# A gated recurrence on one core: the first input, state and biases come in two transfers instead of six, and the input products move one step later

## The chip, the core and the metric

The kernel runs on one core of a Trainium2 chip. Its time is the device time of one execution in microseconds (us). The profile calls the engines PE (TensorE, with PEld for its weight loads), DVE (VectorE), ACT (ScalarE), POOL (GpSimd) and SP (SyncE, which here only issues transfers).

## The reference, cut to what matters

There are 8 sequences of 512 steps, and 512 features and 512 states, all float32. One step needs the state that the step before it left, so the 512 steps are a chain.

```python
def step(h, x_t):
    fused = sigmoid(concatenate([x_t, h], -1) @ w_W + w_b)      # w_W: 1024 x 1024
    r, z = split(fused, 2, axis=-1)
    m = x_t @ wx_W + wx_b + r * (h @ wh_W + wh_b)               # wx_W, wh_W: 512 x 512
    h_new = z * h + (1 - z) * tanh(m)
    return h_new, h_new
out = x + scan(step, h0)                                        # over the 512 steps
```

The names in the kernel: r is the gate that multiplies the state's product, z the gate that keeps the old state. `x` is 8 x 512 x 512, and `h0` (called `cond_1024` in the inputs) is 8 x 512.

## The kernel before

**Layout.** The 512 units stand as four quarters of 128 partitions. The state is kept twice, as half A (quarters 0 and 1) and half B (quarters 2 and 3), in the tiles `hTA` and `hTB`, eight of each in turn. A product has 32 columns of state or of x as its stationary side and a row block of weights as its moving side, so four of them, for j = 0 to 3, fill the 128 partitions of one PSUM bank. Such a set of four is one "piece" below.

**The h side.** Each step i makes six pairs of pieces, in the order `ORDER = "R0 R1 G0 G1 R2 R3 G2 G3 H0 H1 H2 H3"`: R, G and H are three PSUM banks (with a second set for the next group), and the digit is the quarter of the state. The weights are `wgr` (for R and G) and `whh` (for H). DVE then transposes the banks into the state's layout (`turned`, `turn_h`; lines 292 and 310), ACT applies the sigmoids and the tanh (line 192), and DVE forms the new state by scans (line 272). Half A of the new state is ready before half B. POOL adds x and writes the output tile (line 375), and SP stores it every 16 steps.

**The x side.** The products of x don't depend on the state. Four steps make a group (`GS = 4`), and `prefill(g)` makes the group's four pieces (k = 0 to 3, from `wx`) into one of two PSUM banks `xps[g % 2]`, which `seed(g)` on ACT has filled with the biases before. `spread` copies the parts of `xps` into the banks R, G and H of the coming group (ACT, line 217), and `turn_x` transposes the part that belongs to `x_t @ wx_W` (DVE, line 222). Both run during the four steps of group g for group g + 1: at step s of a group, `turn_x(g + 1, s)` and the s-th of `spread`'s copies, or `seed(g + 3)` where s is 3, are the last things that DVE and ACT do. The pieces of `prefill(g + 2)` are made one per step, after the H products, where PE would otherwise wait for half A of the new state:

```python
        if s == 0:
            pre = prefill(g + 2) if g + 2 < NG else iter(())
        ...
        if i:
            take(pre, 1)
```

**The start.** Step 0 is special. Its x products are made in full before it (`both[0]`), and its R and G products go straight into `xps[0]` as one product called Q, 256 columns wide. Group 1's four x pieces are put between them: `FIRST = "Q0 x Q1 Q2 x Q3 x x H0 H1 H2 H3"`. The first piece of group 2 follows at the end of step 0. A bias product (`ones` times `rows4`) adds the biases to both `xps` banks, and DVE copies one of them into the SBUF tile `bias` (line 237), from which `seed` takes them later. Ahead of this PE makes six small products of zeros (tile `none`) and two 128 x 512 products of zeros, one into each `xps` bank; these set the banks' start.

**The transfers of the start.** ACT issues x of the first eight steps (`load_x(0, 0)`), h0 (`hin`), and four rows of biases, six in all. SP issues `wx` in four parts (3.1 MB together), `wgr` in four (2.1 MB), `whh` in two (1.0 MB), the second eight steps of x, and then the next chunks of 16 steps. In the instruction listing each transfer has one of eight completion semaphores, given out in turn, and a transfer that gets a semaphore which an earlier one still uses waits on its issuing engine until that one has landed.

The scheduling is by hand (`manual_schedule`): every engine runs its instructions in the order of the program's text.

Of the kernel before, what the change touches and what calls it, by code (L numbers as in the profile page):

```python
# [7 lines left out]
F32 = mybir.dt.float32  # L8
# [5 lines left out]
P = 128  # L14
NQ = 4
GS = 4
B = 8
# [8 lines left out]

ORDER = "R0 R1 G0 G1 R2 R3 G2 G3 H0 H1 H2 H3"

FIRST = "Q0 x Q1 Q2 x Q3 x x H0 H1 H2 H3"

BANKS = ("R", "G", "H")

# [4 lines left out]
def tile_cond_rnn_residual(  # L37
    ctx: ExitStack,
    tc: tile.TileContext,
    x: bass.AP,  # L40
    h0: bass.AP,
    wx_d: bass.AP,
    wgr_d: bass.AP,
    whh_d: bass.AP,
# [31 lines left out]
    nc = tc.nc  # L76
    NCH = x.shape[0]
    T = NCH * TC
    NG = T // GS

    const = ctx.enter_context(tc.tile_pool(name="const", bufs=1))
# [4 lines left out]

    xins = {}

    def load_x(c, half=slice(0, 2)):

        if c < NCH:
            if c not in xins:
                xins[c] = xin_p.tile([P, 2, NQ, TC * B // 2], F32, tag="xin", name=f"xin_{c}")
            (nc.scalar if half == 0 else nc.sync).dma_start(
                out=xins[c][:, half], in_=x[c].rearrange("p (e k n) -> p e k n", e=2, k=NQ)[:, half]
            )

    def x_of(c, k, t, n):

        e, t = divmod(t, TC // 2)  # L100
        return xins[c][:, e, k, t * B : (t + n) * B]

    load_x(0, 0)

    rows4 = const.tile([P, 512], F32, name="rows4")
    nc.vector.memset(rows4, 0.0)
    for j in range(NQ):
        nc.scalar.dma_start(out=rows4[32 * j : 32 * j + 1], in_=bias_d[j : j + 1])
    hin = const.tile([P, NQ, B], F32, name="hin")
    nc.scalar.dma_start(out=hin, in_=h0)  # L110

    wx = const.tile([P, NQ, NQ, 384], F32, name="wx")
    for k in range(NQ):
# [2 lines left out]
    wgr = const.tile([P, NQ, NQ, 256], F32, name="wgr")  # L116
    for k in range(NQ):
        nc.sync.dma_start(out=wgr[:, k], in_=wgr_d[:, k])
    whh = const.tile([P, NQ, NQ, 128], F32, name="whh")
# [3 lines left out]
    def wh(bank, k, j):  # L123
        return whh[:, k, j] if bank == "H" else wgr[:, k, j, {"G": slice(0, 128), "R": slice(128, 256), "Q": slice(0, 256)}[bank]]

    load_x(0, 1)

    def pair(n, name, rows, slots):
# [13 lines left out]
    zeros = const.tile([P, 512], F32, name="zeros")  # L142
# [4 lines left out]
    ones = const.tile([P, NQ, 32], F32, name="ones")  # L147
# [21 lines left out]
    xps = [psum.tile([P, 512], F32, name=f"xp{q}") for q in range(2)]  # L169

    def mm(out_, lhsT, rhs, start=False):
        nc.tensor.matmul(  # L172
            out_, lhsT, rhs, start=start, stop=False, skip_group_check=True
        )


    for t_ in list(banks[0].values()) + list(banks[1].values()):
        mm(t_, none[:, :128], none, start=True)
    for t_ in xps:
        mm(t_, zeros[:, :128], zeros, start=True)  # L180
    for hf in range(2):
        for slot in (0, 2):
            nc.vector.tensor_copy(
# [14 lines left out]
    def seed(g):  # L198

        nc.scalar.copy(xps[g % 2], bias)  # L200

    def prefill(g):

        c, t0 = divmod(g * GS, TC)
        for k in range(NQ):
            for j in range(NQ):
                mm(
                    xps[g % 2][32 * j : 32 * j + 32, 64:448],
                    x_of(c, k, t0, GS),
                    wx[:, k, j, :],  # L210
                )
            yield

    def spread(g, names):

        for n in names:
            nc.scalar.copy(banks[g % 2][n], xps[g % 2][:, XP[n]])  # L217
# [8 lines left out]
    def take(it, n=None):  # L226
        while n is None or n > 0:
            if next(it, it) is it:
                return
            n = None if n is None else n - 1  # L230

    both = [prefill(g) for g in range(2)]
    take(both[0], 2)
    for t_ in xps:
        mm(t_, ones.rearrange("p j m -> p (j m)"), rows4)
    bias = const.tile([P, 512], F32, name="bias")
    nc.vector.tensor_copy(bias, xps[1])
    take(both[0])
    spread(0, "RGH")
    for e in range(NQ):  # L240
        turn_x(0, e)
# [2 lines left out]
    for i in range(T):  # L244
        g, s = divmod(i, GS)
        c, t = divmod(i, TC)
        ps = banks[g % 2]
        if t == 0 and c > 0:
            load_x(c + 3)
        if t == 0:  # L250
            ot = out_p.tile([P, TC, NQ, B], F32, tag="ot", name=f"ot_{c}")
        if s == 0:
            pre = prefill(g + 2) if g + 2 < NG else iter(())

        for n in (ORDER if i else FIRST).split():
            if n == "x":
                take(both[1], 1)
                continue
            bank, k = n[0], int(n[1])
            hs = hT[k // 2][i % NH][:, :, k % 2, 2]  # L260
            for j in range(NQ):
                to = xps[0][:, :256] if bank == "Q" else ps[bank]
                mm(to[32 * j : 32 * j + 32, :], hs, wh(bank, k, j))
        if i:
            take(pre, 1)

        rows = slice(B * s, B * s + B)

# [77 lines left out]
        if i == 0:  # L346

            seed(2)
            take(pre, 1)
        if i == T - 1:  # L350
            nc.gpsimd.tensor_tensor(
                ot[:, t, :2, :].rearrange("p c n -> p n c"),
                x_of(c, slice(0, 2), t, 1).rearrange("p c n -> p n c"),
                state(0, T),
                ALU.add,
            )
# [17 lines left out]
        def add(hf, engine):  # L374
            return engine.tensor_tensor(  # L375
                ot[:, t, 2 * hf : 2 * hf + 2, :].rearrange("p c n -> p n c"),
                x_of(c, slice(2 * hf, 2 * hf + 2), t, 1).rearrange("p c n -> p n c"),
                state(hf, i + 1),
                ALU.add,
            ).ins  # L380
# [84 lines left out]
```

## Time and profile before

| | |
|---|---|
| median of 3 runs | 1697.41 us (1697.31 to 1697.63) |
| the profiled execution, its own time | 1697.74 us |
| its span, first to last instruction | 1695.9 us |
| busy: PE, PEld, DVE, ACT, POOL | 1683.5, 1463.7, 1093.9, 927.1, 231.1 us |
| moved by DMA | 30.86 MB, mean 18 GB/s |
| mean granted TensorE clock | 0.998 of full |
| first R product of step 1 | 24.11 us after the span's start |

All places in time below are microseconds from the start of the span. Between the span and the execution's own time lie 1.84 us that the profile doesn't show. In the chain of waits an entry is "start, length, what"; in the timeline it is "start, length, engine, line, operation, output and input, count", and a bracket at its end tells how long the engine stood idle before it and what ended that. The windows view gives, for each stretch, its length, PE's busy time, the number of PE's instructions, the granted TensorE clock as a share of full speed, the mean busy share of the 16 DMA engines, and GB/s.

### The profile page before, as it was taken

Reading aid. Unit: us, or ns where it says so; the run is one execution under the profiler, and the core shown is the slowest. Engines: PE = TensorE matmul, PEld = TensorE weight load, DVE = VectorE, ACT = ScalarE, POOL = GpSimd, SP = SyncE. Lnnn points to the kernel's source line nnn. Section 1 sums busy time; section 2 is a strip of 40 time slices with the busy share of each in tenths; the row PEclk is TensorE's granted clock in tenths of the full one; section 3 lists DMA queues with packets and bytes.
Section 4 is the critical chain, followed back from the end, with each engine's and each line's share of the span. In section 5 each row is a group of like instructions: output and inputs, shape, how many; then the busy total and the mean of one; then the engine's idle time right before and its main releaser. Section 6 shows DMA issues by size and latency. Waiting matters only on the chain.

```text
span 1695.9 us, 121388 instructions
## 1 busy us (share of the span) xinstructions
PE 1683.5 (99%) x53230; PEld 1463.7 (86%) x53230; DVE 1093.9 (65%) x8229; ACT 927.1 (55%) x5120; POOL 231.1 (14%) x1032
## 2 busy tenths in 40 slices
PE   8999999999999999999999999999999999999998
PEld 5888888888888888888888888888888888888887
DVE  4666666666666666666666666666666666666666
ACT  3555555555555555555555555555555555555554
POOL 0111111111111111111111111111111111111111
PEclk9999999999999999999999999999999999999999
DMA  4000000000000000000000000000000000000000
GB/s 176 17 4 17 17 17 17 12 9 17 17 17 17 5 17 17 17 17 4 17 18 17 17 10 11 17 17 17 17 4 17 17 17 17 4 17 11 11 11 10
DMA packets 11628, 30.86 MB, mean 18 GB/s; under 512 B 1364, under 2 KB 1876, under 8 KB 11096
## 3 DMA queue, kind: packets, MB, share of 16 engines
q1 hardware_dynamic: 10800, 22.94, 4.1%
q8 instruction: 416, 6.82, 1.7%
q14 instruction: 116, 0.95, 0.2%
q10 hardware_dynamic: 296, 0.16, 0.0%
HBM read 14.70 MB, written 8.39 MB: 14 GB/s over the span
## 4 chain that ended last, share of the span: by engine, by line
PE 98%; DMA 1%; DVE 0%; ACT 0%; issue 0%; SPq 0%
PE R L172 26%; PE G L172 26%; PE H L172 26%; PE xp L172 20%; DMA wx<-in_wx_dram 0%; DMA xin<-in_x_dram 0%; DVE md1A L310 0%; DVE hTA L272 0%; ACT hd0A L192 0%; ACT hTA L192 0%; DVE tz L292 0%; DVE md1A L222 0%; SPq L114 0%; ACT hTB L192 0%; ACT R L217 0%
## 5 line engine op out<-in xcount | busy, mean ns | idle before, releaser
L172 PE MATMUL xp<-wx,xin 128*32 128x384 f32 x4096 | 439.1, 488 | 2.4 <-DMA wx<-in_wx_dram 2.4
L172 PEld LDWEIGHTS R<-wgr,hTA 128*32 128x32 f32 x8176 | 243.5, 136 | 211.4 <-DVE hTA L272 211.0
L292 DVE STREAM_TRANSPOSE tr<-R 128x64 f32<-128x64 f32 x1022 | 194.4, 229 | 301.8 <-PE R L172 301.8
L172 PE MATMUL R<-wgr,hTA 128*32 128x128 f32 x8176 | 330.4, 273 | 2.6 <-DVE hTA L272 2.6
L172 PE MATMUL H<-whh,hTA 128*32 128x128 f32 x8192 | 330.7, 273 | 0.0
L172 PE MATMUL H<-whh,hTB 128*32 128x128 f32 x8192 | 330.7, 273 | 0.0
L172 PE MATMUL R<-wgr,hTB 128*32 128x128 f32 x8176 | 330.1, 273 | 0.0
L172 PE MATMUL G<-wgr,hTB 128*32 128x128 f32 x8176 | 330.1, 273 | 0.0
L172 PE MATMUL G<-wgr,hTA 128*32 128x128 f32 x8176 | 330.0, 273 | 0.0
L375 POOL TENSOR_TENSOR ot<-xin,hTB 128x16 f32<-128x16 f32 x511 | 127.7, 250 | 1457.2 <-DVE hTB L272 1362.4
L192 ACT ACTIVATE hd0B<-tz 128x16 f32<-128x16 f32 x512 | 115.5, 226 | 306.0 <-DVE tz L292 306.0
L172 PEld LDWEIGHTS H<-whh,hTA 128*32 128x32 f32 x8192 | 260.3, 136 | 0.3 <-issue 0.3
L172 PEld LDWEIGHTS G<-wgr,hTA 128*32 128x32 f32 x8176 | 259.7, 136 | 0.0
L192 ACT ACTIVATE md0A<-tr 128x16 f32<-128x16 f32 x512 | 120.8, 236 | 253.3 <-DVE tr L292 253.3
L172 PEld LDWEIGHTS H<-whh,hTB 128*32 128x32 f32 x8192 | 253.4, 122 | 0.0
L172 PEld LDWEIGHTS G<-wgr,hTB 128*32 128x32 f32 x8176 | 252.9, 122 | 0.0
L172 PEld LDWEIGHTS R<-wgr,hTB 128*32 128x32 f32 x8176 | 238.3, 122 | 0.1
L272 DVE TENSOR_TENSOR_SCAN hTA<-hd0A,hTA 128x48 f32<-128x48 f32 x512 | 132.1, 258 | 150.8 <-ACT hTA L192 150.8
L272 DVE TENSOR_TENSOR_SCAN hTB<-hd0B,hTB 128x24 f32<-128x24 f32 x1024 | 158.2, 196 | 103.0 <-ACT hTB L192 103.0
L192 ACT ACTIVATE hd0A<-tz 128x16 f32<-128x16 f32 x512 | 119.0, 232 | 110.8 <-DVE tz L292 110.8
L310 DVE STREAM_TRANSPOSE md1A<-G 128x64 f32<-128x64 f32 x511 | 160.6, 314 | 28.7
L192 ACT ACTIVATE hTB<-hTB 128x16 f32<-128x16 f32 x512 | 121.4, 237 | 82.3 <-DVE hTB L272 79.3
(58 smaller groups left out, 1679.1 us busy)
## 6 DMA issues: line engine op xcount, KB each, us to landing
xin<-in_x_dram SPq DMA_DIRECT2D x31, 256.0 KB, 3.8
out_dram<-ot SPq DMA_DIRECT2D x31, 256.0 KB, 2.9
wx<-in_wx_dram SPq DMA_DIRECT2D x4, 768.0 KB, 6.1
wgr<-in_wgr_dram SPq DMA_DIRECT2D x4, 512.0 KB, 8.6
whh<-in_whh_dram SPq DMA_DIRECT2D x1, 768.0 KB
whh<-in_whh_dram SPq DMA_DIRECT2D x1, 256.0 KB
out_dram<-ot SPq DMA_DIRECT2D x1, 192.0 KB
xin<-in_x_dram ACTq DMA_DIRECT2D x1, 128.0 KB, 5.2
```

The source lines that it names most:

```text
L172: nc.tensor.matmul(out_, lhsT, rhs, start=start, stop=False, skip_group_check=True)
L192: inst = nc.scalar.activation(out_, in_, func, **kw).ins
L272: nc.vector.tensor_tensor_scan(*[t_[:, :, c_].rearrange("p n c s -> p (n c s)") for t_ in (out_, d0, d1)], 0.0, ALU.mult, ALU.add,)
L292: inst = nc.vector.transpose(t_.rearrange("p c n -> p (c n)"), raw[n][hf]).ins
L310: nc.vector.transpose(md1[hf][g % 2][:, :, :, 0].rearrange("p n c -> p c n"), raw["h"][hf])
L375: return engine.tensor_tensor(ot[:, t, 2 * hf : 2 * hf + 2, :].rearrange("p c n -> p n c"), x_of(c, slice(2 * hf, 2 * hf + 2), t, 1).rearr ...
```

## The change

Six things are edited.

1. x of the first eight steps and h0 are packed side by side in one DRAM tensor `xh` and come in one transfer into a tile `head`. The products and the output additions of these steps read `head`.
2. The four rows of biases come in one transfer into partitions 0, 32, 64 and 96 of `rows4`.
3. The bias product goes into `xps[0]` alone, ahead of the x products, and starts that bank. DVE copies it to `bias` from there, and `seed(1)`, on ACT, copies the biases into `xps[1]`.
4. The two products of zeros in front both go into `xps[1]`; a third one (`warm()`) stands after group 0's x products.
5. In step 0 one x piece is taken out of `FIRST`, and it is the one piece at the end of the step. All x pieces now come from one sequence, `x_side()`: group g + 2's pieces are made at steps 4g + 1 to 4g + 4 instead of 4g to 4g + 3.
6. All transfers of `load_x` are issued by SP.

```diff
-FIRST = "Q0 x Q1 Q2 x Q3 x x H0 H1 H2 H3"
+FIRST = "Q0 x Q1 Q2 Q3 x x H0 H1 H2 H3"
...
+    NX = NQ * TC * B // 2
+    head = const.tile([P, NX + NQ * B], F32, name="head")
+    nc.scalar.dma_start(out=head, in_=xh)
+    hin = head[:, NX:].rearrange("p (k b) -> p k b", k=NQ)
...
-            (nc.scalar if half == 0 else nc.sync).dma_start(
+            nc.sync.dma_start(
...
         e, t = divmod(t, TC // 2)
+        if c == 0 and e == 0:
+            first = head[:, :NX].rearrange("p (k n) -> p k n", k=NQ)
+            return first[:, k, t * B : (t + n) * B]
         return xins[c][:, e, k, t * B : (t + n) * B]
 
-    load_x(0, 0)
 
     rows4 = const.tile([P, 512], F32, name="rows4")
     nc.vector.memset(rows4, 0.0)
-    for j in range(NQ):
-        nc.scalar.dma_start(out=rows4[32 * j : 32 * j + 1], in_=bias_d[j : j + 1])
-    hin = const.tile([P, NQ, B], F32, name="hin")
-    nc.scalar.dma_start(out=hin, in_=h0)
+    nc.scalar.dma_start(out=rows4[0:128:32], in_=bias_d)
...
-    for t_ in xps:
-        mm(t_, zeros[:, :128], zeros, start=True)
+    def warm():
+
+        mm(xps[1], zeros[:, :128], zeros)
+
+    mm(xps[1], zeros[:, :128], zeros, start=True)
+    warm()
+    mm(xps[0], ones.rearrange("p j m -> p (j m)"), rows4, start=True)
+    bias = const.tile([P, 512], F32, name="bias")
+    nc.vector.tensor_copy(bias, xps[0])
...
-    both = [prefill(g) for g in range(2)]
-    take(both[0], 2)
-    for t_ in xps:
-        mm(t_, ones.rearrange("p j m -> p (j m)"), rows4)
-    bias = const.tile([P, 512], F32, name="bias")
-    nc.vector.tensor_copy(bias, xps[1])
-    take(both[0])
+    def x_side():
+        for g in range(1, NG):
+            yield from prefill(g)
+
+    seed(1)
+    take(prefill(0))
+    warm()
+    later = x_side()
...
-        if s == 0:
-            pre = prefill(g + 2) if g + 2 < NG else iter(())
...
-                take(both[1], 1)
+                take(later, 1)
...
-        if i:
-            take(pre, 1)
+        take(later, 1)
...
             seed(2)
-            take(pre, 1)
```

More of the change, by code (lines that the diff above doesn't have):

```diff
@@ L40, in tile_cond_rnn_residual @@
     x: bass.AP,
-    h0: bass.AP,
+    xh: bass.AP,
     wx_d: bass.AP,
@@ L446 @@
     xd = c_(xd).reshape(NCH, 128, 4 * TC * Bn)
-    h0_d = c_(units(f["cond_1024"].T))
+    h0 = units(f["cond_1024"].T).reshape(128, 4 * Bn)
+    xh_d = c_(_np.concatenate([xd[0, :, : 2 * TC * Bn], h0], 1))
     nc = _bacc.Bacc("TRN2", target_bir_lowering=False, num_devices=1)
@@ L451 @@
     for name, a in (
-        ("x", xd), ("h0", h0_d), ("wx", wx_d), ("wgr", wgr_d), ("whh", whh_d), ("bias", bias_d),
+        ("x", xd), ("xh", xh_d), ("wx", wx_d), ("wgr", wgr_d), ("whh", whh_d), ("bias", bias_d),
     ):
```

## The prediction

> **What bounds the kernel now.** I read the page first: PE is busy 99% of the span, and its chain is "PE 98%; DMA 1%". In the timeline one step with its x piece takes 3.27 us of uninterrupted PE work (R starts at 1663.16 and 1666.43), so 512 steps are about 1670 us, which the change does not shorten. What it touches is the start, so next I read the chain of waits, its first 25 us (start, length, what):
>
> ```profile
> 0.74 5.23 DMA xin<-in_x_dram
> 5.99 0.33 SPq L114
> 6.36 7.07 DMA wx<-in_wx_dram
> 13.47 1.30 PE xp L172 x8
> 15.42 0.34 DVE md1A L222 x2
> 16.03 6.75 PE xp L172 x64
> 22.78 0.87 PE H L172 x32
> 23.65 0.64 PE xp L172 x8
> ```
>
> The last part of `wx` is issued only at 6.36, after the transfer of x, and lands at 13.43; then PE works through group 0's last piece and step 0, and step 1's R begins at 24.11 (timeline). Who made SP wait is in the waits of SP's queue (total, times, longest):
>
> ```profile
> SPq L114 <- DMA xin<-in_x_dram: 4.4, 1, 4.4
> SPq L118 <- DMA hin<-in_h_dram: 1.1, 1, 1.1
> ```
>
> By the instruction listing the third part of `wx` needs the completion semaphore that x's transfer holds: eight semaphores, and x, two parts of `wx`, h0 and four bias rows have all eight. The windows show what that does (fourth column the clock, last GB/s):
>
> ```profile
> 6.00:7.00 1.00, 1.00 (x9) 1.00 0.89 354
> 7.00:8.00 1.00, 0.75 (x12) 1.00 0.95 139
> 8.00:9.00 1.00, 1.00 (x9) 1.00 0.89 362
> 13.00:14.00 1.00, 0.53 (x8) 0.89 0.95 361
> 14.00:15.00 1.00, 0.75 (x8) 0.50 0.98 401
> 20.00:21.00 1.00, 1.00 (x16) 0.70 1.04 391
> ```
>
> The queue runs dry at 7 to 8. And PE, waiting for `wx`, loses half its clock from about 13.8 (0.89 of that window) to 20.6 (0.70).
>
> **Two transfers for six.** In the changed listing x with h0, the bias rows, four `wx` and two `wgr` parts share the eight semaphores, so all of `wx` is issued without a wait; the ninth, `wgr` part 2, waits for x, with some 3 MB queued ahead of it. What stays behind on SP's queue is the rest of `wgr`, `whh` and the later x, each waiting for a transfer long queued. The gain: issue plus time to landing gives 7.7 for `wx` part 1, 5.99 + 5.6 = 11.6 for part 2, 13.4 for part 3. Part 2 took 3.9 us after part 1, part 3 took 1.8 after part 2, at equal size. Without the dry queue part 2 should take 1.8 as well: 2.1 us saved, for all that lies behind. Bounds: at least the bytes missing in window 7 to 8, (400 - 139) of 400 GB/s, 0.65 us, if the late landings come from slow queues and not from the restart; at most 2.9, if also `wgr` part 0 (13.4 to 7.89 + 7.5 = 15.4, where parts 1 to 3 average (9.5 + 9.6 - 15.4)/3 = 1.2) loses its extra 0.8. I take 2.1, since parts 2 and 3 differ in nothing but the restart.
>
> So `wx` is complete at 11.3 instead of 13.4. `wgr` part 3 landed at 19.1, the second x at 11.6 + 10.4 = 22.0; between them 1.18 MB in 2.9 us, so `whh` part 0 was at 21.0 and part 1 at 21.7. After: `wgr` at 13.3, 14.5, 15.8 and 17.0, `whh` at 18.9 and 19.6.
>
> A rule of the Trainium skill speaks against this gain: "DMA: Bandwidth & Descriptors", section "Issuing engines are not separate DMA queues", says that transfers of all engines share the same 16 DMA engines and that spreading their issue saves only issuing time. By it the merge would be worth at most ACT's issue time, which no engine on the chain waits for: the sum would be left with the x piece below, 0.6 us. The 4.4 us wait on a semaphore's earlier user is another cost than that, so I go by the row.
>
> **Step 0.** With `wx` at 11.3, group 0's last piece takes 0.85 (row at 11.64, full clock); from its end to the first Q lie 1.29 (14.74 to 16.03: three copies, four transposes), so Q0 starts at about 13.5. At full clock Q pieces are 0.43 and x pieces 0.64: Q0 and x to 14.6, Q1 to 15.0, Q2 waits for its weights to 15.8, Q3 to 17.0 and ends at 17.4, two x pieces to 18.7, H waits for `whh` to 18.9 and its last quarter to 19.6. That quarter is 0.22 (of 0.87 for H), the x piece behind it 0.64: R of step 1 at 20.5 instead of 24.11. **3.6 us** gained. Here arrival of weights is what is late next; PE is not. So the x piece taken out of step 0 and the better clock are not added: they are what makes room for the weights to show. The state's path has slack: from Q3's end to half A of the new state it took 1.8 us (21.3 to 23.08), so 19.2, before 20.5.
>
> **Bias first.** The bias product now stands ahead of the x pieces on PE, and DVE's copy of it, 0.69, ahead of both h0 copies and of the first x piece, which must wait for it since it writes the same bank. The rows' landing isn't shown: x, ahead of them on ACT's queue, landed at 5.97, h0 behind it at 7.9. I take 6.4, where PE ends the zeros (2.69 + 3.72), because the rows now follow x directly: product 1.2, copy 0.7, three x pieces 1.9, so 10.2, and 1.1 us spare before 11.3. At 7.9 it would be 11.6, 0.3 late, hidden again by Q2's wait. Cost nothing; without that cover up to 0.9.
>
> **The zeros.** Two 128x512 zero products as before, hidden as before (PE waited for x). The third one, 0.85 to 1.86, lies in the 1.29 us between the last x piece and Q0: nothing at full clock, 0.6 at half, also ahead of Q2's wait. `seed(1)` on ACT, 0.59, is due by 12 and can run at 9. Nothing.
>
> **The x side one step later.** Step 504 gets a piece: steps without one last 3.23 (1669.60 to 1672.83), so **0.04** is lost. Every group's last piece now ends shortly before `turn_x` reads it on DVE, with ACT's copy of R and POOL's output additions behind: piece ends at 1643.79, `turn_x` ran at 1644.33, 0.54 spare. Nothing, unless that is used up. The bank's `seed` gets a step more.
>
> **Sum.** Span 1695.9 - 3.6 + 0.04 = 1692.3; with the 1.84 around it 1694.2; the profiled execution was 0.33 above the median, so the median should be 1693.8. A difference of about 0.2% (3.4 us) is what a measurement of this kernel can tell from no change, and the forecast lies just beyond it.
>
> **The rivals.** *The late queues stay late* (chance 0.11): only 0.65 us of arrival comes back, `whh` ends at 21.05, R starts at 21.9, gain 2.2 less 0.04: 1695.3. For it: `wgr` part 0 was slow without any dry queue. Against: parts 1 to 3 then ran evenly.
>
> *The clock falls in another stretch* (0.07). Before, a stretch of 3.4 us up to 13.8 with PE about a third busy ended at half clock, and one about 60% busy did not end it. After, 10.4 to 13.8 is about half busy, 13.8 to 17.2 as well. If the first drops the clock, the second is then full (Q and x at double length end at 17.2) and nothing is lost. If only the second does, 17.2 to 20.6 runs at half: two x pieces 2.6, H 1.2, R at 22.1, gain 2.0: 1695.4. "TensorE: Matmul & The Clock Gate", section "What's actually happening", has windows of 3.4 us and half clock only after an idle one; the 6.8 us in the trace are two of them, but a third of a window busy did not save the clock here, so the trace decides. By the page alone this rival could not happen.
>
> *Slower: DVE waits for the late piece* (0.06). `turn_x` stands in order before DVE's next transposes; if its piece ended over 0.54 us later than I read (a piece that waits, or a modelled end), 127 groups would each lose the excess, less the 0.6 us that DVE idles next. At an excess of 0.7, 0.1 x 127 = 13 us less the gain: 1707. Against: PE has no waits in these steps.
>
> **How the numbers follow.** The forecast has 0.76: from 1692.9 (weights 2.9 us earlier, so R at 19.7 and a gain of 4.4, and 0.1 more, as the lowest run lies 0.1 under the median) to 1694.8 (weights 1.1 us earlier, gain 2.6). Of it I give 0.66 to below 1694.0, as 2.1 is the mid of its bounds, and 0.10 to between. The range, 1692.9 to 1695.6, takes in the two smaller gains. Faster 0.66; same 0.10 + 0.11 + 0.07 = 0.28; slower 0.06.
>
> **What would show it.** Right: SP's first wait is at `wgr`, no window between 3 and 20 falls below 200 GB/s, `wx` lands near 11.3, R of step 1 starts near 20.5, steps keep 3.27. Wrong: a part of `wx` landing after 12.5; half clock past 18; DVE waits at `turn_x` in each group; R of step 1 bounded by PE rather than `whh`.

## The result, and the profile after

| | before | after |
|---|---|---|
| median of 22 runs | 1697.39 us | 1694.68 us |
| ratio | | 0.9985, 95% interval 0.9978 to 0.9992 |
| profiled execution: own time, span | 1697.74, 1695.9 us | 1694.75, 1693.0 us |
| R of step 1 starts | 24.11 us | 20.75 us |

The kernel is faster by 2.7 us, 0.15%. One of the 22 executions of the kernel before took 6329 us and stands outside the ratio. The first R product of step 1, before and after (timelines):

```profile
24.11 0.63 PE L172 MATMUL R<-wgr,hTA 128*32 128x128 f32 x16
20.75 0.62 PE L177 MATMUL R<-wgr,hTA 128*32 128x128 f32 x16
```

The chain of waits of the changed kernel, its first 21 us (start, length, what):

```profile
0.74 5.16 DMA head<-in_xh_dram
5.92 0.33 SPq L123
6.29 10.94 DMA wgr<-in_wgr_dram
17.27 1.95 PE xp L177 x24
19.22 1.07 PE H L177 x32
20.29 0.65 PE xp L177 x8
```

`wx` has left the chain. The wait for x's semaphore is still there (1.8 us in the waits of SP's queue), but the transfer that stands behind it is now part 2 of `wgr` (issued at 5.9, landed at 16.0), and the part issued next, the last of `wgr`, lands at 17.2. Meanwhile the queue has other parts to move. The windows:

```profile
6.00:7.00 1.00, 0.70 (x2) 1.00 1.02 424
7.00:8.00 1.00, 0.99 (x2) 1.00 1.05 442
11.00:12.00 1.00, 0.67 (x8) 1.00 0.96 233
14.00:15.00 1.00, 1.00 (x20) 1.00 1.03 418
20.00:21.00 1.00, 1.00 (x31) 1.00 0.87 326
```

The dry stretch at 7 to 8 is gone (442 instead of 139 GB/s), and no window from 14 to 21 shows half clock. (The first event of the clock is at 7.1 us in this trace; before it the view shows 1.00, although the products run at half speed.) One dip is left, 233 GB/s at 11 to 12, where part 0 of `wgr` is on its way. PE's timeline shows how step 0 now goes:

```profile
11.34 0.85 PE L177 MATMUL xp<-wx,head 128*32 128x384 f32 x8 [0.42 <-DMA wx<-in_wx_dram]
13.61 0.67 PE L177 MATMUL xp<-wgr,hTA 128*32 128x256 f32 x8 [0.37 <-DMA wgr<-in_wgr_dram]
17.27 0.66 PE L177 MATMUL xp<-wgr,hTB 128*32 128x256 f32 x8 [0.60 <-DMA wgr<-in_wgr_dram]
19.61 0.68 PE L177 MATMUL H<-whh,hTB 128*32 128x128 f32 x16
20.11 0.83 PE L177 MATMUL xp<-wx,head 128*32 128x384 f32 x8
```

The last piece of group 0 starts when `wx` is complete, at 11.34; every Q then starts when its part of `wgr` has landed. The last part of `whh` (issued at 7.6, 12.2 to landing) is there at 19.8, and R starts 0.95 behind it; before, R stood 2.4 behind it (21.7 and 24.11).

### The profile page after: what moved, and what is told of

Read it like the earlier page. It is cut to its first block, busy times and chain, and to the rows that moved or that the text cites. A ratio compares the mean times of both kernels' runs of the same rounds, so it can differ in the third digit from the quotient of the medians.

```text
span 1693.0 us, 121258 instructions
## 1 busy us (share of the span) xinstructions
PE 1681.5 (99%) x53230; PEld 1468.8 (87%) x53230; DVE 1087.5 (64%) x8229; ACT 916.6 (54%) x5121; POOL 230.3 (14%) x1032
## 4 chain that ended last, share of the span: by engine, by line
PE 98%; DMA 1%; DVE 0%; ACT 0%; issue 0%; SPq 0%
PE R L177 26%; PE G L177 26%; PE H L177 26%; PE xp L177 19%; DMA wgr<-in_wgr_dram 1%; DMA head<-in_xh_dram 0%; DVE md1A L320 0%; DVE hTA L282 0%; ACT hd0A L204 0%; ACT hTA L204 0%; DVE tz L302 0%; SPq L123 0%; ACT hTB L204 0%; DVE hTB L282 0%; ACT hd0B L204 0%
## 5 line engine op out<-in xcount | busy, mean ns | idle before, releaser
L177 PE MATMUL xp<-wx,xin 128*32 128x384 f32 x4032 | 432.4, 486 | 0.0
L177 PEld LDWEIGHTS R<-wgr,hTA 128*32 128x32 f32 x8176 | 248.9, 135 | 205.2 <-DVE hTA L282 204.7
L177 PEld LDWEIGHTS R<-wgr,hTB 128*32 128x32 f32 x8176 | 246.5, 122 | 0.0
L320 DVE STREAM_TRANSPOSE md1A<-G 128x64 f32<-128x64 f32 x511 | 157.1, 307 | 28.7
## 6 DMA issues: line engine op xcount, KB each, us to landing
whh<-in_whh_dram SPq DMA_DIRECT2D x1, 256.0 KB, 12.2
```

Source lines behind the costliest of these rows:

```text
L177: nc.tensor.matmul(out_, lhsT, rhs, start=start, stop=False, skip_group_check=True)
L320: nc.vector.transpose(md1[hf][g % 2][:, :, :, 0].rearrange("p n c -> p c n"), raw["h"][hf])
```

## The experiments

The theory: the gain is the earlier arrival of the weights, since SP issues all of `wx` without waiting for a completion semaphore. The rivals: fewer transfers are cheaper in themselves; PE's new order and its clock make the gain. All times are medians of 10 or 11 runs; the intervals of the ratios are about 0.09% to each side, or 1.5 us, so that medians tell a gain of 2.5 us from none, and smaller differences are read in the profiles, from one execution each. The three columns on the right are places in the profile, in us.

| kernel | median, us | ratio to before, interval | `wx` complete | last of `whh` | R of step 1 |
|---|---|---|---|---|---|
| merge alone | 1694.97 | 0.9986 (0.9977 to 0.9995) | 11.2 | 20.1 | 21.31 |
| PE's order alone | 1696.55 | 0.9996 (0.9987 to 1.0005) | 13.6 | 21.8 | 22.69 |
| no late zeros | 1694.78 | 0.9986 (0.9977 to 0.9995) | 11.3 | 19.9 | 20.89 |
| x side back | 1695.09 | 0.9988 (0.9979 to 0.9997) | 11.4 | 20.1 | 21.27 |
| small ones by POOL | 1694.43 | 0.9984 (0.9975 to 0.9993) | 11.3 | 19.0 | 21.86 |
| wait put back | 1696.99 | 0.9998 (0.9989 to 1.0007) | 13.8 | 21.7 | 22.68 |
| piece inside | 1694.62 | 0.9985 (0.9976 to 0.9995) | 11.3 | 20.1 | 20.37 |
| late loads | 1694.38 | 0.9983 (0.9974 to 0.9992) | 11.9 | 19.4 | 21.40 |
| one zero | 1695.29 | 0.9988 (0.9979 to 0.9997) | 11.2 | 20.0 | 20.96 |
| three zeros | 1695.02 | 0.9986 (0.9977 to 0.9995) | 11.4 | 20.2 | 21.18 |
| zeros and late loads | 1694.37 | 0.9982 (0.9973 to 0.9991) | 11.4 | 19.8 | 20.78 |

**The merge alone, and PE's order alone.** The first is the kernel before with `head` and the one bias transfer of the diff above and nothing else; the second is the changed kernel with this undone:

```diff
-    nc.scalar.dma_start(out=head, in_=xh)
+    load_x(0, 0)
...
-    nc.scalar.dma_start(out=rows4[0:128:32], in_=bias_d)
+    for j in range(NQ):
+        nc.scalar.dma_start(out=rows4[32 * j : 32 * j + 1], in_=bias_d[j : j + 1])
+    hin = const.tile([P, NQ, B], F32, name="hin")
+    nc.scalar.dma_start(out=hin, in_=h0)
```

> The kernel before, with only its transfers changed (x with h0 in one, the four bias rows in one); PE's, ACT's and DVE's orders stay as before. Arrival theory (all that counts is that the parts of wx are issued without a wait): wx complete near 11.3 us and whh near 19.8 as in the changed kernel, no window between 4 and 20 us under 200 GB/s; PE's clock may fall for one stretch (13.8 to 17.2), R of step 1 starts at 20.9 to 21.4 (changed kernel 20.75, before 24.1), so 2.6 to 3.0 us under the kernel before. Rival, PE's order and clock theory: arrival moves but PE works off step 0 at half clock until 20.6, R of step 1 at 22.5 to 23, at most 1.5 us under before.

> The changed kernel with the six transfers of before: only PE's order, the bias copy and the zeros are changed. Arrival theory: wx complete at 13.4 and whh at 21.7 as before, so R of step 1 can't start before 22.5, and the gain is at most 1.5 us, and that comes from the clock, which the late zeros bring back at 17.2 instead of 20.6. PE's order and clock theory: R of step 1 at 20.8 to 21.5, most of the 2.7 us. If neither acts without the other: no gain, R at 24.

The merge alone keeps 2.8 of the 3.4 us at step 1's R and most of the time (2.25 us under the kernel before, which had 1697.22 beside it). PE's order alone brings R forward by 1.4 in its profile, and its time, 0.7 under before, can't be told from no change. Its R waits for `whh` to land at 21.8, as expected. In the merge alone no stretch of half clock came, though PE stood idle for most of 12 to 14. In PE's new order R starts 0.94 to 0.95 behind the last of `whh` in five profiles (the changed kernel, PE's order alone, no late zeros, one zero, three zeros), with `whh` landing anywhere from 19.8 to 21.8: there the landing sets R.

**The wait put back.** Both transfers stay merged; one wait is added.

```diff
         inst = nc.sync.dma_start(out=wx[:, k], in_=wx_d[:, k]).ins
+        if k == 2:
+            tc.add_manual_dep(inst, head_in.name, SYNC)
```

> The changed kernel, both transfers merged, with one wait put back: the third part of wx is issued only when x and h0 have landed, at 5.9 us. Semaphore theory: the queue runs dry at 7 to 8 us again (a window under 250 GB/s), wx complete at 13.0 to 13.5, whh at 21.3 to 21.8, R of step 1 at 22.2 to 22.7, so 1.4 to 1.9 us of the span's 2.9 us gain are lost and it stands with the run of PE's order alone. Rival, fewer transfers are the gain: wx near 11.3 to 12, R at 20.7 to 21.3.

The waits of SP's queue in this kernel (total us, count, longest us):

```profile
SPq L119 <- DMA head<-in_xh_dram: 4.2, 1, 4.2
```

Its windows (GB/s last):

```profile
7.00:8.00 1.00, 1.00 (x2) 1.00 0.73 147
```

And PE's timeline:

```profile
13.82 0.85 PE L179 MATMUL xp<-wx,head 128*32 128x384 f32 x8 [1.17 <-DMA wx<-in_wx_dram]
22.68 0.62 PE L179 MATMUL R<-wgr,hTA 128*32 128x128 f32 x16
```

The 4.2 us wait, the dry window and the late `wx` are back together, R is 1.9 us later than in the changed kernel, and the gain in time can't be told from none. So the wait is the cause, not the number of transfers. R is still 1.4 earlier than before, as with PE's order alone.

**Six transfers without the wait.** The kernel before, its small transfers issued elsewhere.

```diff
-        nc.scalar.dma_start(out=rows4[32 * j : 32 * j + 1], in_=bias_d[j : j + 1])
+        nc.gpsimd.dma_start(out=rows4[32 * j : 32 * j + 1], in_=bias_d[j : j + 1])
...
-    nc.scalar.dma_start(out=hin, in_=h0)
+    nc.gpsimd.dma_start(out=hin, in_=h0)
```

> The kernel before with its six transfers, of which the five small ones (h0 and four bias rows) are issued by POOL, so that they hold none of the eight completion semaphores that SP's transfers use. Semaphore theory: SP issues all four wx parts without a wait, wx complete near 11.3 us, whh near 20, R of step 1 at 21.2 to 21.5 as in the run with the merge alone, 2.3 to 2.8 us under before. Rival, the number of transfers itself costs (each small one holds up the DMA engines): wx later than 12.5, R after 22.5, less than 1.5 us under before.

The other half of the proof: six transfers, no wait ahead of `wx`, and the whole gain in time. R came 0.4 later than expected, though `whh` was the earliest of all; the profiled execution, 1695.62, is the slowest of the 11. PE's timeline shows what for:

```profile
18.90 0.62 PE L172 MATMUL H<-whh,hTB 128*32 128x128 f32 x16
21.21 0.85 PE L172 MATMUL xp<-wx,xin 128*32 128x384 f32 x8 [1.69 <-ACT R L217]
```

The x piece at the end of step 0 stood idle for 1.7 us. ACT's copy, named as releaser, had long been done; the piece reads the second eight steps of x (`xin`), and that transfer's last part landed at 21.1 in this execution (issued at 9.5, 11.6 to landing).

**The x side.** Back to its old steps, and, as a contrast, with the extra piece inside step 0 but none at its end.

```diff
 # x side back
-FIRST = "Q0 x Q1 Q2 Q3 x x H0 H1 H2 H3"
+FIRST = "Q0 x Q1 Q2 x Q3 x x H0 H1 H2 H3"
-        take(later, 1)
+        if i:
+            take(later, 1)
...
             seed(2)
+            take(later, 1)
 # piece inside: the same without the last added line
```

> The changed kernel with the x pieces back at their old steps: a fourth x piece inside step 0, and group g+2's pieces at steps 4g to 4g+3. Arrival theory: the extra piece (0.65 us) fills PE's wait for wgr's last part, R of step 1 stays within 0.15 us of 20.75, step 504 gets its 0.04 us back, time the same within what can be measured. Rival, PE bounds step 0: R of step 1 0.65 us later, 21.4.

> The changed kernel with group 1's last x piece inside step 0, between Q2 and Q3, and no piece at the end of step 0; group 2's pieces stay at steps 1 to 4. Theory that the late landing of the second x made the old place of the x side cost 0.5 us: here nothing at the end of step 0 reads it, PE fills its wait for wgr with the piece, and R of step 1 starts at 20.0 to 20.2 right behind H; then it waits for half B of the state, so that R of step 2 is 0 to 0.2 us earlier than in the changed kernel. Rival, PE bounds step 0 (the extra piece costs its 0.65 us): Q3 starts 0.4 or more later than 17.3, and R of step 2 is 0.3 or more later.

The first expectation failed in its number: R at 21.27, 0.5 late. But the rival's reason isn't it either, as the second kernel shows (PE's timeline; the first two lines are of the kernel with the x side back, the others of the one with the piece inside):

```profile
20.63 0.85 PE L177 MATMUL xp<-wx,xin 128*32 128x384 f32 x8
21.27 0.65 PE L177 MATMUL R<-wgr,hTA 128*32 128x128 f32 x16
17.29 0.66 PE L177 MATMUL xp<-wgr,hTB 128*32 128x256 f32 x8
20.37 0.62 PE L177 MATMUL R<-wgr,hTA 128*32 128x128 f32 x16
21.72 0.66 PE L177 MATMUL R<-wgr,hTB 128*32 128x128 f32 x16 [0.29 <-DVE hTB L283]
24.20 0.62 PE L177 MATMUL R<-wgr,hTA 128*32 128x128 f32 x16
```

With the extra piece inside, Q3 still starts at 17.29 (17.27 in the changed kernel), so the piece is hidden. R follows H at once, 0.2 later than expected with `whh` 0.3 later than in the changed kernel, and half B of the state then ends the wait; step 2 starts at 24.20 in both kernels.

Of the 0.5 us with the x side back, 0.34 is `whh`, which landed that much later in this execution (20.14 against 19.80), and not the order. The rest, 0.2, is the order: the piece at the end of step 0 belongs to group 2 and reads the second x, which lands last, at 20.5, so it starts at 20.63, where 0.3 behind `whh`, as in the changed kernel, would have been 20.45. By the same reckoning it is 0.3 in the merge alone. In the new order that place has a group 1 piece, which reads `head`. So moving the x side by a step takes a wait for a transfer off the path, of 0.2 to 0.3 us where the second x lands 0.35 to 0.5 behind `whh`, and of 1.7 where it lands 2.0 behind, as in the profile with POOL's transfers.

**The zeros.** The late product removed; one product in front instead of two; three instead of two.

```diff
 # no late zeros
     take(prefill(0))
-    warm()
 # one zero
     mm(xps[1], zeros[:, :128], zeros, start=True)
-    warm()
 # three zeros
     warm()
+    warm()
```

> The changed kernel without the product of zeros behind group 0's x pieces. Arrival theory: PE has room, R of step 1 stays at 20.7 to 21.0 even if the granted clock falls to half from 13.8 to 17.2, time within 0.3 us of the changed kernel. Clock theory: the clock falls at 13.8 and comes back only at 20.6, R of step 1 at 22 or later, 1.3 us or more above the changed kernel.

> The changed kernel with one product of zeros in front instead of two, so that PE stands idle from about 4.6 us until the bias rows land at 6.6. Clock theory (with the bias product first, it is the zeros up to the rows' landing that bring the clock up at 7 to 8): the granted clock is not up before 10, more likely 14.5 as in two earlier traces where PE stood idle before the bias product; group 0's x pieces take 1.3 us each, Q0 starts near 16, R of step 1 at 21.2 to 21.6, 0.5 to 0.7 us later than in the changed kernel. Arrival theory alone: R stays at 20.7 to 20.9, as PE has room.

> The changed kernel with three products of zeros in front, so that PE is busy until 7.5 to 8.3 whatever the rows' landing. Clock theory: the clock is up by 7 to 8 in every execution; bias product about 1 us later, group 0's last piece at 11.4 at the earliest as before, R of step 1 at 20.6 to 20.9; the median at or up to 0.3 us under the changed kernel, with fewer of its runs above 1695. If the zeros only delay: group 0's last piece at 12 or later and R still at 20.7 to 20.9, since wgr and whh arrive later than PE needs them.

The late product does nothing that shows: without it the clock held too, R is 0.14 later with `whh` 0.14 later, and the time stays. With one product in front PE stood idle for 2.0 us before the bias product, and the x pieces were slow, as expected, but the clock was back by 12.3, and R came only 0.2 later, as much as `whh` did; its median is 0.6 higher than the changed kernel's, within the interval. Three products brought nothing: R at 21.18, since `whh` happened to end at 20.2.

**The later loads.** x for steps 16 to 63, behind `whh` on SP's queue, is issued only after the output additions of steps 1 to 3; then the same with three zeros in front.

```diff
-        if i < 3:
-            load_x(i + 1)
+        if 2 <= i < 5:
+            tc.add_manual_dep(load_x(i - 1).ins, pool_done[i].name, SYNC)
```

> The changed kernel with the loads of x for steps 16 to 63 issued after the output additions of steps 1 to 3 instead of behind whh. Theory that PE's 0.2 us halt in step 1 (at 22.8 to 23.1) is a late fetch of its instructions beside these loads: the halt is gone, step 1 lasts 3.27 instead of 3.45, the span is 0.1 to 0.2 us shorter. Rival, the halt has nothing to do with them: step 1 lasts 3.4 or more, span as in the changed kernel.

> Three products of zeros in front, and the loads of x for steps 16 to 63 after the output additions of steps 1 to 3. Expected best of the two: clock up by 8, whh at 19.4 to 19.8, R of step 1 at 20.3 to 20.7, span 1692.6 to 1692.9, median 1694.0 to 1694.5, 0 to 0.7 us under the changed kernel. If the late loads don't matter: as with the three zeros alone.

The first expectation was about a halt of 0.18 us in step 1 of the changed kernel. It was absent here, but it was absent as well in seven of the kernels above, with the early loads, so this says nothing on its cause. In the profiled execution of the first of the two, PE's clock came up late:

```profile
6.99 2.05 PE L177 MATMUL xp<-rows,ones 128*128 128x512 f32 x2 [0.59 <-DMA rows<-in_bias_dram]
9.82 5.06 PE L177 MATMUL xp<-wx,head 128*32 128x384 f32 x32 [0.78 <-DVE bias L192]
21.40 0.65 PE L177 MATMUL R<-wgr,hTA 128*32 128x128 f32 x16
```

The bias rows landed 0.3 and `wx` 0.6 later than in most profiles, PE idled 0.6 us, and everything up to 14.5 ran at half speed (2.05 for the bias product where the kernel with three zeros has 1.02). R is 0.65 late although `whh` was complete at 19.4: here PE is what is late. So the bias product, whose cost I put at nothing, is covered only thinly. With the loads moved, `whh` was complete at 19.4 and 19.8; in the seven profiles with its last part ahead of the same early loads and all of `wx` unhindered it was 19.8 to 20.2 (the kernel with POOL's transfers, 19.0, has another queue). The last kernel has the lowest median, 1694.37 (0.01 under the later loads alone), and all its 11 runs lie between 1693.98 and 1694.54, where the changed kernel's lie between 1693.92 and 1696.14. Its ratio's interval overlaps that of the changed kernel, so it beats the kernel before, but that it beats the changed one is not shown.

## Why the prediction was right, and where it was not

**The cause held.** The wait on x's semaphore, the dry queue and the 2.1 us between them are what the change removed: `wx` complete at 11.3 (forecast 11.3), `wgr` at 13.5 to 17.2 (13.3 to 17.0), `whh` at 19.8 (19.6). Neither end of the bounds that I gave, 0.65 to 2.9, came: the late queues did not stay late, and `wgr` part 0 kept its extra time (2.2 us behind `wx`, where the other parts took 1.25). The wait put back and POOL's transfers show the mechanism from both sides. By the rule of the Trainium skill that the prediction cites ("DMA: Bandwidth & Descriptors", section "Issuing engines are not separate DMA queues": issuing from several engines saves only issuing time) 0.6 us would have been left, by the prediction's own reckoning. The gain measured is well over it. The kernel with POOL's transfers shows why: what its edit took away was the wait for a completion semaphore, and `wx` was complete 2.1 us earlier.

**The size came out smaller, 2.7 instead of 3.6,** inside the range but within 0.2% and not beyond it, where I had given 0.66 to beyond; the likeliest case was a little too good. By the profiles, 3.36 of the 3.6 came at step 1's R: `whh` was 0.2 later than forecast. Then 0.18 went in a halt of PE in step 1, between two groups of H's weight loads, and 0.16 in two steps near 1281 us that lasted 3.37 and 3.32; step 504's 0.04 came as said. That is 3.36 - 0.18 - 0.16 - 0.04 = 2.98, and the spans differ by 2.98 in the traces. The halts were no term of my sum at all: their cause is open (the profile says "issue"), and most other profiles lack them, while that of the kernel without the late zeros has four such steps (0.27 in all), so nothing ties them to the change. The last 0.3 are the choice of executions: the profiled one of before lay 0.35 above its median, that of the changed kernel 0.07.

**What I overlooked: the kernel before does not always lose its clock.** I worked the sum out from one profile, in which PE runs at half clock from 13.8 to 20.6 and the mean clock is 0.998. Beside the experiments the kernel before ran 93 times: 37 executions have 0.998 and a median of 1697.87, 24 have 1.000 and a median of 1696.58, 1.3 less, and the other 32, at 0.999, lie between (1697.05). An estimate from the profiles agrees: R starts 0.78 behind the second x in the three kernels whose last piece waits for it (the merge alone, the x side back, POOL's transfers), so at full clock before would have had it at 22.07 + 0.78 = 22.85 instead of 24.11. All ten kernels with `wx` early have 0.999 or 1.000 in all their 119 executions. So against the executions at 1.000 the gain is 1.9 us, about what `whh` gained (21.71 to 19.80). By this reckoning the other 0.8 of the 2.7 is a loss of clock that no longer comes, and 1.3 of the 3.4 at R in the profile is the same. It stays a reckoning: the mean clock doesn't tell where in the span it was lost; only a profile does.

**The x side was mis-sized:** I put the move at nothing in step 0. It is worth 0.2 to 0.3 us at R where I compared it, and 1.7 in one profile, since the old last piece waits for the second x. I had that landing in hand, 22.0 - 2.1 = 19.9, 0.3 behind `whh`, and did not ask which x the piece reads.

**The clock:** once it was up, the clock did not fall again in the profile of any kernel with `wx` early until the last two us or so, with or without the late zeros, so that rival is not borne out. "TensorE: Matmul & The Clock Gate", section "What's actually happening", has a free-running window. Here the ramp, the half clock with which every profile begins, ended at 5.3 to 8.0 us in ten traces, so its phase differs between executions, as the page says; in the three traces where PE had idled 0.6 to 2.0 us ahead of the bias product it ended at 12.3 to 14.9.

**Slower** did not show: steps last 3.265 as before, and DVE does not wait at `turn_x`.

## What to carry to other kernels

Look at the waits of the issuing queue itself: a transfer that waits for a free completion semaphore can leave the queue dry, and what helped here was to free the semaphores (merge small transfers, or issue them where they use others), not to move fewer bytes. When arrival is what bounds a start, list for each product which transfer it reads and put those that read early ones into the waits. And a gain at the start of a long chain is kept only as far as nothing later gives it back: add up the steps to the end before believing it. Look at the clock of all executions, and not only of the profiled one, before taking a stretch of half clock as the rule.

## What the runs showed of the hardware that was not expected

A dry queue costs more than the missing issue time: after it the first packets of `wx` part 2 took 0.9 us each where later ones took 0.23; at the very start they took 0.9 too. Two or three of the 16 shares of a transfer end late, by 0.3 us in the parts of `wx` and by 0.9 in `whh` (18.9 and 19.8 in the changed kernel), and a wait ends with the last share. The dip at 11 to 12 us, 221 to 250 GB/s in eight kernels with `wx` early, was absent in two (369 with POOL's transfers, 412 with the late loads), and its cause stays open.
